# A two-layer graph network on one core: one group a step, PE's results read later, layer 1 summed in a PSUM bank

## The chip, the cores and the metric

The kernel runs on one core of a Trainium2 chip. The metric is device time in microseconds (us), the median of the runs. Engines are named as in the profile: PE (TensorE), PEld (its weight loads), DVE (VectorE), ACT (ScalarE), POOL (GpSimd), SP (SyncE, which here only issues DMAs).

## The reference

A graph has 12,500 nodes with 48 features and 200,000 edges sorted by destination. All numbers are float32.

```python
# layer 0
x_i, x_j = x[dst], x[src]
h = relu(concatenate([x_i, x_j, edge_attr_32], axis=1) @ W1 + b1)   # 128 hidden
msg = h @ W2 + b2                                                    # 48
x = layernorm(x + segment_sum(msg, dst))
# layer 1
m = relu(x[src] + edge_attr_48)
x = layernorm(x + (1 + eps) * x + segment_sum(m, dst))
```

## The kernel before, in words

The edges are cut into 391 groups of 512 (128 partitions x 4 tiles), and two groups make a pair; there are 196 pairs. A group's destinations lie close together, since the edges are sorted: a window of 48 nodes, with a start that is worked out on the chip, holds them all (should one fall outside, `check_windows` raises a flag and a general path runs; it doesn't here). The nodes are cut into 14 segments of 896.

In both layers POOL fetches the rows `x[src]` with indirect DMAs, one for each tile of 128 edges: `gather`, L187, 1564 times a layer.

Layer 0, for a pair `p`:
- `fetch0`: 8 gathers into `cat`, which has per edge 48 columns for a one-hot row, 48 for `x[src]`, 32 for the edge's features.
- `fill0`: ACT copies the edge features into `cat` (L391), DVE writes the one-hot rows (L276: which of the window's 48 nodes is this edge's destination), SP loads for each group the 48 rows of `x @ W1[0:48]` of its window (computed by `project`) into `wcat` (L394). So one matmul gives all three parts of the first linear layer.
- `turn0`: PE transposes the tiles of `cat` into PSUM tile `pt` (L402), DVE copies it to `cat_t` (L404).
- `hidden0`: PE multiplies `cat_t` by `wcat` into `ph` (L412), ACT adds the bias and applies relu (L416).
- `message0`: PE multiplies by W2 into `pm` (L423), DVE adds the bias and writes `msg` (L425).
- `sum0`: PE multiplies `msg` with the one-hot rows into `pa` (L309, 4 tiles added up for each group); `add0`: DVE adds `pa` into the segment's sums `agg` at a column read from a register (L302).

Layer 1, for a pair: `fetch1` gathers from the table of layer 0's results into `xs`; `fill1` writes the one-hot `hot` (L276) and loads edge features; `message1` adds on DVE (`m`, L491) and applies relu on ACT (L493); `sum1` and `add1` as in layer 0.

When a segment's last group has been added, `finish0` or `finish1` adds the overlaps of neighbouring segments, transposes the sums on PE (`px`, L325), and computes the layer norm on DVE and ACT; SP stores the result. Layer 1's gathers wait for all of layer 0's stores.

The order of the work is written out by hand. `run` (L438) goes through steps `k`; in each step it calls the listed stages, a stage with number `d` for pair `k - d`. Every engine executes its instructions in this order. Layer 0's list (L471) holds, with their numbers, fetch (-3), fill (-1), `message0` (1), `turn0` (0), `sum0` (1), `add0` (1), `hidden0` (0). So within one step DVE reads `pm` and `pt`, ACT reads `ph` and DVE reads `pa`, each as soon as PE has written it. In layer 1 (L508) `message1`, `sum1` and `add1` all have number 0. PSUM tiles are single (`bufs=1`); `cat` and `xs` have six buffers of a pair each, `hot` and the messages two, `wcat` four. A gather into a buffer waits until the buffer's last reader is done: `sum0` (PE) in layer 0, `m` (DVE) in layer 1.

```python
    run(
        [(fetch1, -AHEAD), (fill1, -1), (message1, 0), (sum1, 0), (add1, 0)],
        add1, finish1, lead1,
    )
```

Of the kernel before, what the change touches and what calls it, by code (L numbers as in the profile page):

```python
# [51 lines left out]
PAIRS = -(-NCHUNK // 2)  # L53
AHEAD = 3
NW = 4
EC = 6
# [3 lines left out]


def groups(p):
    return range(2 * p, min(2 * p + 2, NCHUNK))
# [27 lines left out]
def gnn_kernel(  # L91
# [18 lines left out]
    with ExitStack() as fast:  # L110
# [4 lines left out]
        min_val=0, max_val=2 * P,  # L115
# [5 lines left out]
def windowed(ctx, tc, dram, flag, x, src, dst, e32, e48, w1, b1, w2, b2, eps, out):  # L121
    nc = tc.nc
    const = ctx.enter_context(tc.tile_pool(name="const", bufs=1))
    cats = ctx.enter_context(tc.tile_pool(name="cats", bufs=AHEAD + 3))
    echunk = ctx.enter_context(tc.tile_pool(name="echunk", bufs=3))
    work = ctx.enter_context(tc.tile_pool(name="work", bufs=2))
    aggs = ctx.enter_context(tc.tile_pool(name="aggs", bufs=3))
    node = ctx.enter_context(tc.tile_pool(name="node", bufs=2))
    seg = ctx.enter_context(tc.tile_pool(name="seg", bufs=3))
    psum = ctx.enter_context(tc.tile_pool(name="psum", bufs=1, space=bass.MemoryType.PSUM))  # L130
# [52 lines left out]

    a_dram = [dram.tile([SROWS, HID], F32, name=f"a{s}", tag=f"a{s}") for s in range(NSEG)]
# [31 lines left out]

    begin.close()

    def check_windows():
        flat = rel.rearrange("p g t -> p (g t)")  # L220
        most = node.tile([P, 1], F32, name="most")
        nc.vector.tensor_reduce(most, flat, AX.X, ALU.max)
        least = node.tile([P, 1], F32, name="least")
        nc.vector.tensor_reduce(least, flat, AX.X, ALU.min)
        over = node.tile([P, 1], F32, name="over")
        nc.vector.tensor_scalar(over, most, float(W), None, op0=ALU.is_ge)
        bad = node.tile([P, 1], F32, name="bad")
        nc.vector.scalar_tensor_tensor(bad, least, 0.0, over, op0=ALU.is_lt, op1=ALU.add)
        pf = psum.tile([1, 1], F32, name="px")
        nc.tensor.matmul(pf, bad, ones[:P, 0:1], start=True, stop=True)  # L230
        nc.vector.tensor_copy(flag, pf)
# [27 lines left out]
    def load_edges(name, table, width, p):  # L259

        c, g = divmod(2 * p, EC)
        if g == 0:
            n = min(EC, NCHUNK - c * EC)
            chunk[name] = echunk.tile([P, EC * TPC, width], F32, name=name)
            nc.sync.dma_start(
                chunk[name].rearrange("p (c t) d -> p c (t d)", t=TPC)[:, :n, :],
                table[c * CHUNK * EC : (c * EC + n) * CHUNK, :].rearrange(
                    "(c p t) d -> p c (t d)", p=P, t=TPC
                ),
            )  # L270
        return chunk[name][:, g * TPC : (g + len(groups(p))) * TPC, :]

    def one_hot(o, p):
        n = len(groups(p)) * TPC
        r = rel.rearrange("p g t -> p (g t)")[:, 2 * p * TPC : 2 * p * TPC + n]
        nc.vector.tensor_tensor(  # L276
            o, iota_w[:, None, :].to_broadcast([P, n, W]),
            r[:, :, None].to_broadcast([P, n, W]), op=ALU.is_equal,
        )
# [4 lines left out]
    def start_of(engine, layer, g):  # L284
        if (engine, layer, g // 4) not in starts_of:
            kind = {nc.sync: mybir.EngineType.SP, nc.vector: mybir.EngineType.DVE}[engine]
            _, starts_of[engine, layer, g // 4] = nc.values_load_multi_w_load_instructions(
# [4 lines left out]
        return starts_of[engine, layer, g // 4][g % 4]  # L292
# [3 lines left out]
    def add_window(layer, g, pa):  # L296
        s = seg_of(g)
        if (layer, s) not in agg:
            agg[layer, s] = aggs.tile([D, SROWS], F32, name="agg")
            nc.vector.memset(agg[layer, s], 0.0)  # L300
        cols = agg[layer, s][:, bass.ds(start_of(nc.vector, layer, g), W)]
        nc.vector.tensor_tensor(cols, cols, pa, op=ALU.add)  # L302

    def reduce_tiles(p, hot, msg):
        pa = psum.tile([D, 2, W], F32, name="pa")
        for i, g in enumerate(groups(p)):
            for j in range(TPC):
# [414 lines left out]
```

## Time and profile before

| | |
|---|---|
| runs | 4828.99, 4833.04 (median), 4858.2 us |
| the profiled execution's own time | 4849.45 us |
| its span | 4847.7 us |
| busy, of the span | PE 41%, PEld 31%, DVE 19%, ACT 9%, POOL 63% |
| first gather of layer 0, of layer 1, end of the last gather | 7.57, 2556.8, 4832.6 us |
| granted TensorE clock, 80 to 2600 us and 2600 us to the end | 0.69, 0.50 of full speed |

The page of the profile gives for each group of instructions: line, engine, operation, output and inputs by the program's names, shapes and count; then busy time and mean duration in ns; then the engine's idle time just before these instructions and what ended most of it ("issue": nothing that the profile shows; "remote": a semaphore whose writer the profile could not tell). In the timeline a row has start, duration, engine, line and operation, and in brackets the idle time before it. Busy time of PE is modelled. A row of windows has the stretch, its length, the busy time with the count, the granted clock, the DMA engines' share and GB/s. A row of waits has the engine and line that waited, whom for, the total in us, the number of times and the longest.

### The profile page before, as it was taken

The numbers are of one execution on the slowest core, as the hardware profiler recorded it, in microseconds if no ns is written. First come the engines' busy times: TensorE is split into PE (matmuls) and PEld (weight loads), VectorE is DVE, ScalarE is ACT, GpSimd is POOL, SyncE is SP. The second block draws the span as 40 slices with busy tenths as digits, with TensorE's granted clock in tenths as the row PEclk, the third lists the DMA queues.
The fourth block names the chain that finished last, engine by engine and source line by source line (L and its number), as shares of the span: only waits on it lengthen the run. The fifth ranks groups of instructions, "written<-read, shape, count | busy, mean of one in ns | idle before, by whom it ended". The sixth has DMA issues, their size and how long they took to land.

```text
span 4847.7 us, 37626 instructions
## 1 busy us (share of the span) xinstructions
PE 2000.8 (41%) x12224; PEld 1503.6 (31%) x12224; DVE 925.0 (19%) x2082; ACT 434.8 (9%) x702; POOL 3073.4 (63%) x3136
## 2 busy tenths in 40 slices
PE   4666666666667667666660111011111110111011
PEld 2454555444445445454540111011011110111011
DVE  1222222222222222222220111112111111121112
ACT  1111111111111111111110000000000000000000
POOL 6556665656655666655646766667666766676666
PEclk7767676766766666767675555555555555555555
DMA  2111111111111111111111121112111211221121
GB/s 50 34 37 36 30 40 37 30 36 37 30 37 37 33 37 37 30 37 36 30 27 37 30 44 38 33 28 45 40 31 30 46 39 19 43 44 39 18 44 35
DMA packets 296027, 172.52 MB, mean 36 GB/s; under 512 B 111040, under 2 KB 295568, under 8 KB 295824
## 3 DMA queue, kind: packets, MB, share of 16 engines
q0 software_dynamic: 100096, 77.07, 10.7%
q1 hardware_dynamic: 178832, 84.31, 6.4%
q10 hardware_dynamic: 16896, 8.69, 0.6%
q8 instruction: 97, 1.59, 0.1%
q14 instruction: 106, 0.87, 0.1%
HBM read 157.20 MB, written 12.62 MB: 35 GB/s over the span
## 4 chain that ended last, share of the span: by engine, by line
another core or an unknown queue 43%; PE 28%; issue 13%; DVE 5%; POOL 5%; ACT 3%; DMA 1%; DVEq 1%; ACTq 0%; SPq 0%; POOLq 0%
PE ph L412 9%; PE pm L423 7%; PE pa L309 6%; POOL xs L187 4%; PE pt L402 4%; ACT h L416 2%; DVE cat_t L404 1%; DVE m L491 1%; DVE agg L302 1%; PE px L243 1%; DVE msg L425 1%; PE px L325 1%; DVE cat L276 1%; ACT msg L493 0%
## 5 line engine op out<-in xcount | busy, mean ns | idle before, releaser
L187 POOL DMA_INDIRECT cat<-in_x_dram,src_i x1564 | 1521.5, 973 | 985.2 <-issue 973.9
L187 POOL DMA_INDIRECT xs<-x_dram,src_i x1564 | 1550.2, 991 | 773.4 <-issue 445.2
L309 PE MATMUL pa<-hot,msg 128*48 128x48 f32 x3128 | 296.3, 282 | 1821.0 <-issue 1116.1
L309 PEld LDWEIGHTS pa<-hot,msg 128*48 128x48 f32 x3128 | 264.8, 192 | 1852.5 <-issue 1134.7
L423 PE MATMUL pm<-w_sb,h 128*128 128x48 f32 x3128 | 530.8, 338 | 372.4 <-ACT h L416 233.6
L423 PEld LDWEIGHTS pm<-w_sb,h 128*128 128x128 f32 x3128 | 502.1, 252 | 576.9 <-ACT h L416 355.9
L412 PE MATMUL ph<-cat_t,wcat 128*128 128x512 f32 x782 | 546.6, 836 | 115.6 <-issue 66.1
L302 DVE TENSOR_TENSOR agg<-agg,pa 48x48 f32 x782 | 153.6, 196 | 2118.2 <-remote 1621.7
L416 ACT ACTIVATE h<-ph,b_sb 128x1024 f32<-128x1024 f32 x196 | 217.9, 1112 | 1939.6 <-PE ph L412 1400.6
L309 PE MATMUL pa<-cat,msg 128*48 128x48 f32 x3128 | 265.6, 263 | 270.1 <-DVE msg L425 207.7
L425 DVE TENSOR_TENSOR msg<-pm,b_sb 128x384 f32<-128x384 f32 x196 | 109.1, 556 | 1391.6 <-remote 543.4
L309 PEld LDWEIGHTS pa<-cat,msg 128*48 128x48 f32 x3128 | 236.8, 175 | 331.7 <-DVE msg L425 226.2
L402 PE MATMUL pt<-ident,cat 128*128 128x128 f32 x1564 | 328.8, 381 | 2.0 <-ACT cat L391 2.0
L402 PEld LDWEIGHTS pt<-ident,cat 128*128 128x128 f32 x1564 | 290.6, 214 | 2.3 <-ACT cat L391 2.3
L404 DVE COPY cat_t<-pt 128x1024 f32<-128x1024 f32 x196 | 239.0, 1220 | 232.5 <-PE pt L402 117.5
L493 ACT ACTIVATE msg<-m 128x384 f32<-128x384 f32 x196 | 102.2, 521 | 1916.3 <-DVE m L491 1475.8
L412 PEld LDWEIGHTS ph<-cat_t,wcat 128*128 128x128 f32 x782 | 183.1, 260 | 286.0 <-issue 221.3
L276 DVE TENSOR_TENSOR cat<-iota_w,rel 128x384 f32<-128x384 f32 x196 | 109.2, 557 | 36.7 <-issue 36.1
L491 DVE TENSOR_TENSOR m<-xs,e48c 128x384 f32<-128x384 f32 x196 | 106.6, 544 | 39.7 <-issue 19.2
L276 DVE TENSOR_TENSOR hot<-iota_w,rel 128x384 f32<-128x384 f32 x196 | 106.3, 543 | 0.3
L325 PE MATMUL px<-ident,agg 48*128 48x48 f32 x196 | 25.6, 291 | 188.4 <-DVE agg L319 93.1
L391 ACT ACTIVATE cat<-e32c 128x256 f32<-128x256 f32 x196 | 79.6, 406 | 42.6 <-DMA cat<-in_x_dram,src_i 14.7
(53 smaller groups left out, 325.5 us busy)
## 6 DMA issues: line engine op xcount, KB each, us to landing
e48c<-in_e_dram SPq DMA_DIRECT2D x65, 576.0 KB
cat<-in_x_dram,src_i POOLq DMA_INDIRECT x1564
xs<-x_dram,src_i POOLq DMA_INDIRECT x1564
e32c<-in_e_dram SPq DMA_DIRECT2D x65, 384.0 KB
wcat<-a SPq DMA_DIRECT2D x391, 24.0 KB
a<-a ACTq DMA_DIRECT2D x14, 256.0 KB
a<-a ACTq DMA_DIRECT2D x14, 192.0 KB
x_seg<-in_x_dram SPq DMA_DIRECT2D x14, 168.0 KB
```

The source lines that it names most:

```text
L187: nc.gpsimd.indirect_dma_start(out=t, out_offset=None, in_=table, in_offset=bass.IndirectOffsetOnAxis(ap=src_i[:, g * TPC + j : g * TPC + ...
L276: nc.vector.tensor_tensor(o, iota_w[:, None, :].to_broadcast([P, n, W]), r[:, :, None].to_broadcast([P, n, W]), op=ALU.is_equal,)
L302: nc.vector.tensor_tensor(cols, cols, pa, op=ALU.add)
L309: nc.tensor.matmul(pa[:, i, :], msg[:, k, :], hot[:, k, :], start=j == 0, stop=j == TPC - 1)
L402: nc.tensor.transpose(pt[:, k, :], cat[p][:, k, :], ident[:P, :P])
L404: nc.vector.tensor_copy(cat_t[:, :n, :], pt[:, :n, :])
L412: nc.tensor.matmul(ph[:, part_of, :], wcats[g % NW], h[p][:, part_of, :], start=True, stop=True)
L416: nc.scalar.activation(t[:, :n, :], ph[:, :n, :], AF.Relu, bias=b1_sb)
L423: nc.tensor.matmul(pm[:, k, :], h[p][:, k, :], w2_sb, start=True, stop=True)
L425: nc.vector.tensor_tensor(msg[:, :n, :], pm[:, :n, :], b2_sb[:, None, :].to_broadcast([P, n, D]), op=ALU.add)
L491: nc.vector.tensor_tensor(m[:, :n, :], xs[:, :n, :], h[p], op=ALU.add)
L493: nc.scalar.activation(msg[:, :n, :], m[:, :n, :], AF.Relu)
```

## The change

A step now handles one group, not a pair. In layer 0 the stages are split where PE's result is read, and the reader stands one step after PE: `turned0` (DVE copies `pt`), `relu0` (ACT reads `ph`), `bias0` (DVE reads `pm`), `add0` (DVE reads `pa`). `pt`, `ph` and `pm` have two PSUM tiles. `cat` has 14 buffers of one group, `xs` 10, `wcat` 8; the gathers stay six groups ahead in the order, and an edge chunk is five groups instead of six.

In layer 1 the window of a group no longer comes from a register: group `g` gets 128 fixed destinations from `32 g - 48` on (`rel1`), so that neighbouring groups' windows overlap by a known amount. PE adds 12 groups into one PSUM bank of 480 columns: a matmul with zeros opens it, each group's four tiles are added at column `32 i`, a matmul with zeros closes it. `drain1` stands nine steps after the group in the order (eight after its sum): DVE adds the bank's first 96 columns to the ring `table`, ACT copies the other 384. A segment is finished once its columns are complete. `hot` and `msg1` come from a pool of ten buffers. `check_windows` checks both kinds of window.

```diff
-AHEAD = 3
-NW = 4
-EC = 6
+AHEAD = 6
+NW = 8
+EC = 5
+R1 = 48
+GB = 12
...
+W1 = STEP + 2 * R1
+SB = GB * STEP
+BANK = SB + 2 * R1
+RING = 5 * SB
...
-    cats = ctx.enter_context(tc.tile_pool(name="cats", bufs=AHEAD + 3))
+    cats = ctx.enter_context(tc.tile_pool(name="cats", bufs=AHEAD + 8))
     echunk = ctx.enter_context(tc.tile_pool(name="echunk", bufs=3))
-    work = ctx.enter_context(tc.tile_pool(name="work", bufs=2))
+    xs_pool = ctx.enter_context(tc.tile_pool(name="xs_pool", bufs=AHEAD + 4))
+    late = ctx.enter_context(tc.tile_pool(name="late", bufs=10))
+    work = ctx.enter_context(tc.tile_pool(name="work", bufs=3))
...
+    rel1 = const.tile([P, NCHUNK, TPC], F32, name="rel1")
+    nc.vector.tensor_tensor(
+        rel1, dst_g, fixed[:, :, None].to_broadcast([P, NCHUNK, TPC]), op=ALU.subtract
+    )
...
+    def turn0(g):
+        pt[g] = psum.tile([Q, TPC, P], F32, name="pt", bufs=2)
+        for j in range(TPC):
+            nc.tensor.transpose(pt[g][:, j, :], cat[g][:, j, :], ident[:P, :P])
+
+    def turned0(g):
+        h[g] = work.tile([Q, TPC, P], F32, name="cat_t")
+        nc.vector.tensor_copy(h[g], pt.pop(g))
+
+    def hidden0(g):
+        ph[g] = psum.tile([HID, TPC, P], F32, name="ph", bufs=2)
+        nc.tensor.matmul(ph[g], wcats[g % NW], h[g], start=True, stop=True)
+
+    def relu0(g):
+        h[g] = work.tile([HID, TPC, P], F32, name="h")
+        nc.scalar.activation(h[g], ph.pop(g), AF.Relu, bias=b1_sb)
...
     run(
-        [(lambda p: p >= AHEAD and fetch0(p), -AHEAD), (fill0, -1), (message0, 1), (turn0, 0),
-         (sum0, 1), (add0, 1), (hidden0, 0)],
+        [(lambda g: g >= AHEAD and fetch0(g), -AHEAD), (fill0, -2), (add0, 7), (sum0, 6),
+         (bias0, 5), (message0, 4), (relu0, 3), (hidden0, 2), (turned0, 1), (turn0, 0)],
         add0, finish0, lead0,
     )
...
+    def fill1(g):
+        o = late.tile([P, TPC, W1], F32, name="hot")
+        nc.vector.tensor_tensor(
+            o, iota_1[:, None, :].to_broadcast([P, TPC, W1]),
+            rel1[:, g, :, None].to_broadcast([P, TPC, W1]), op=ALU.is_equal,
+        )
+        hot[g] = o
+        h[g] = load_edges("e48c", e48, D, g)
+
+    def message1(g):
+        m = work.tile([P, TPC, D], F32, name="m")
+        nc.vector.tensor_tensor(m, cat.pop(g), h[g], op=ALU.add)
+        msg = late.tile([P, TPC, D], F32, name="msg1")
+        nc.scalar.activation(msg, m, AF.Relu)
+        h[g] = msg
...
+    def sum1(g):
+        k, i = divmod(g, GB)
+        last = i == GB - 1 or g == NCHUNK - 1
+        if i == 0:
+            bank[k] = psum.tile([D, BANK], F32, name="pt", bufs=2)
+            nc.tensor.matmul(bank[k], zeros[:, :D], zeros[:, :BANK], start=True, stop=False)
+        o, msg = hot.pop(g), h.pop(g)
+        for j in range(TPC):
+            nc.tensor.matmul(
+                bank[k][:, i * STEP : i * STEP + W1], msg[:, j, :], o[:, j, :],
+                start=False, stop=False, skip_group_check=True,
+            )
+        if last:
+            nc.tensor.matmul(
+                bank[k], zeros[:, :D], zeros[:, :BANK], start=False, stop=True
+            )
+
+    def drain1(g):
+
+        k, i = divmod(g, GB)
+        if i < GB - 1 and g < NCHUNK - 1:
+            return
+        for first, end in (0, R1), (R1, 2 * R1):
+            at = (k * SB - R1 + first) % RING
+            if k * SB - R1 + first >= 0:
+                both = table[:, at : at + R1]
+                nc.vector.tensor_tensor(both, both, bank[k][:, first:end], op=ALU.add)
...
     run(
-        [(fetch1, -AHEAD), (fill1, -1), (message1, 0), (sum1, 0), (add1, 0)],
-        add1, finish1, lead1,
+        [(fetch1, -AHEAD), (fill1, -2), (sum1, 1), (drain1, 9), (message1, 0)],
+        None, None, lead1,
     )
```

## The prediction

> **What bounds the kernel now.** I read the page's fifth part first, then cut the span at the first and last gather of each layer, then read the waits of layer 1 and the timeline. The costliest rows are the gathers of L187, on POOL:
>
> ```profile
> L187 POOL DMA_INDIRECT cat<-in_x_dram,src_i x1564 | 1521.5, 973 | 985.2 <-issue 973.9
> L187 POOL DMA_INDIRECT xs<-x_dram,src_i x1564 | 1550.2, 991 | 773.4 <-issue 445.2
> ```
>
> The windows of L187 alone (length, busy time and count):
>
> ```profile
> 7.50:2509.10 2501.60, 1521.51 (x1564) 0.70 0.18 35
> 2509.10:2556.80 47.70, 0.00 (x0) 0.83 0.07 15
> 2556.80:4832.60 2275.80, 1550.15 (x1564) 0.50 0.18 36
> 4832.60:4847.70 15.10, 0.00 (x0) 0.50 0.08 16
> ```
>
> So the span is 7.5 + 2501.6 + 47.7 + 2275.8 + 15.1. In the timeline an undisturbed gather takes 0.94 to 0.95 us with 0.30 to the next: 1.25 us each, a floor of 1564 x 1.25 = 1955 us a layer. Layer 0 is 547 above it: 1521.5 - 1564 x 0.945 = 44 are stretched gathers, 2501.6 - 1521.5 - 1564 x 0.305 = 503 are pauses. Layer 1 by the same sums: 72 stretched, 249 paused.
>
> What makes POOL pause? The waits of layer 1:
>
> ```profile
> DVE agg L302 <- remote: 1521.6, 103, 41.6
> ...
> POOL xs L187 <- DVE m L491: 251.7, 38, 17.4
> ```
>
> POOL waits for a free `xs`, which `m` frees; `m` stands behind the window adds (L302) on DVE, and those sit idle up to 41.6 us. "Remote" hides what they wait for: their one wait on another engine is for `pa` from PE. The timeline near the start shows the effect bare:
>
> ```profile
> 50.62 3.65 PE L423 MATMUL pm<-w_sb,h 128*128 128x48 f32 x16 [7.70 <-ACT h L416]
> ...
> 54.06 1.93 PE L402 MATMUL pt<-ident,cat 128*128 128x128 f32 x8
> ...
> 67.29 0.94 POOL L187 DMA_INDIRECT cat<-in_x_dram,src_i  x1 [0.30 <-issue]
> 75.38 0.56 DVE L425 TENSOR_TENSOR msg<-pm,b_sb 128x384 f32<-128x384 f32 x1 [35.44 <-remote]
> 75.85 1.22 DVE L404 COPY cat_t<-pt 128x1024 f32<-128x1024 f32 x1
> ```
>
> `pm` ended at 54.27, its reader starts at 75.38, 7 us after POOL stopped: while gathers stream, PE's completion can reach other engines very late, and a whole burst then arrives at once. Pairing rows of the trace, 101 of 196 pairs in layer 1 have over 2 us between `pa` and its add; in layer 0 `msg` starts 1.7 us after `pm` on average. So: POOL is the floor, late PE results make it pause.
>
> **What the Trainium skill says.** "SBUF — State Buffer", section "SBUF: two separate sides": a DVE operation with two SBUF inputs holds the port pair shared with GpSimd, and a GpSimd operation that reads SBUF is shut out until it ends. The trace agrees:
>
> ```profile
> 3338.41 0.54 DVE L276 TENSOR_TENSOR hot<-iota_w,rel 128x384 f32<-128x384 f32 x1
> 3338.60 1.64 POOL L187 DMA_INDIRECT xs<-x_dram,src_i  x1 [0.30 <-issue]
> 3338.88 0.54 DVE L491 TENSOR_TENSOR m<-xs,e48c 128x384 f32<-128x384 f32 x1
> ```
>
> The gather that starts inside `hot` lasts 1.64, 0.69 more: until `m` ends (3339.42) less 0.12 after its own start. So a gather needs the port 0.12 us after its start, and two DVE operations back to back don't let it in between. "DMA: Bandwidth & Descriptors", section "SWDGE vs HWDGE vs iDMA": GpSimd writes the descriptors of indirect DMAs; no other engine can take this floor away (1.25 us here). "Perfetto Trace Analysis", section "Per-instruction lifecycle": a matmul's shown end is estimated and the semaphore's way isn't shown; 54.27 against 75.38 agrees, though the page says nothing of 20 us. "PSUM — Partial Sum Buffer", section "The four PSUM rules": a matmul that starts a group clears the bank's written marks, later ones add. That is what the zero matmul opens the 480-column bank for; no run shows it yet.
>
> **The change part by part.** *One group a step, layer 0.* The gathers stay 1564. DVE's four operations at half size stand in the groups with shapes kept apart (the odd last pair): one-hot 0.36, `msg` 0.36, `cat_t` 0.69, add 0.20 = 1.61 a group against 2.73 a pair now, 0.24 more a group, 96 us in all; ACT 0.69 + 0.30 against 1.52 a pair, 88 in all. Both lie under POOL (DVE busy 587 and ACT 317 of 2520 us) and cost nothing; without that cover they would cost those sums. PE does the same matmuls: (329 + 547 + 531 + 266)/391 = 4.3 us a group, under 5.0. SP loads the same 391 `wcat`, two steps ahead with eight buffers, and 79 edge chunks in place of 66; nothing waits for SP longer than for POOL. The added constants and the doubled window check (about 2 + 4 us of DVE) lie under the first gathers.
>
> *Results read a step later, two PSUM tiles each.* Step k's PE work needs only step k-1 of DVE and ACT, and these need only step k-1 of PE. The loop is two steps long: step >= (PE 4.3 + DVE 1.6 + hops 0.3 + lateness)/2, so lateness up to 3.8 us costs nothing against 5.0. Where PE is late by more, DVE stalls, but POOL has about six groups (30 us) of `cat` ahead (14 buffers, one freed at step g+6). What is late next: `project` and `finish0`, where PE and ACT or DVE still wait for each other in the same step, some 27 places. I take 60 us of pauses in place of 503; bounds 0 and 310 (5.8 us a group).
>
> *Collisions, layer 0.* One-hot still waits for the fourth gather of its group. Landings come about 2.2 us after a gather's start, the DVE waits add 0.13: it runs from 2.33 to 2.69 while the port is wanted at 2.50 + 0.12. That is 0.07 x 391 = 27, and 15 for the layer norms. Layer 0: 1955 + 27 + 15 + 60 = 2057.
>
> *Between the layers.* 47.7 now. The last group has nine steps to pass instead of two pairs, without POOL beside it: 50.
>
> *Layer 1.* Gone are 782 window adds with their 98 register loads, and every wait for PE in the step. `hot` grows to 512 elements: from 384 at 0.544 and 192 at 0.343, 0.68 us; `m` is 0.36. DVE 1.07 with the drain, against 0.74; hidden as such. PE moves 128 columns where it moved 48, at most 8 x 0.24 = 1.9 us (the slow `pt` rate), and 66 zero matmuls of 1.7 (L211's two rows, nearest in shape); hidden under 5.0. The drain stands eight steps (40 us) behind the last sum. A new wait: `hot` waits for the slot that the sums of seven steps ago read, with `m` behind it on DVE and POOL behind `m`; but 35 us of lateness and then nine `xs` slots lie in between. So I take no pause, bounds 0 and 249.
>
> The price is the port. `m` waits for the fourth gather's landing, `hot` follows at once: from 2.33, `m` takes 0.27 to the next start, `hot` 0.69, end at 3.29. The gather due at 2.50 wants the port at 2.62 and gets it at 3.29: 0.67 a group, locked in phase, 391 x 0.67 = 262. Bounds: 0, if `m` starts only after 2.62, and 0.96 x 391 = 375. Plus 15 for layer norms. Layer 1: 1955 + 262 + 15 = 2232, hardly below its 2276: the pause comes back as collisions.
>
> *Tail.* 15.1 now; now nine steps without work, closing matmul, drain, last segment: 22.
>
> Sum: 7.5 + 2057 + 50 + 2232 + 22 = 4369 of span against 4847.7, -9.9%. The profiled execution's own time is 4849.45, the median of the runs 4833.04, 0.34% lower: 4355.
>
> **Rivals.** *No collisions in layer 1*: landing and waits together last past 2.62, as in one pair of the trace (`m` at 2.76, after four waits in a row; here there are two). 4355 - 262 = 4093, say 4095. Against it: landings of 2.08 to 2.44 in most of the rows I looked at.
> *Late results still stop POOL*: layer 0 at 5.8 us a group (+208), or layer 1 keeps its 249. About 4570. For it: at the start, with POOL streaming without pause, results were 10, 6.5 and 21 us late; against it: with PE at work every 3.6 to 5.8 us (the burst from 3338 on) at most 2.3 us, and PE is busier now.
> *Slower*: the same lateness as a lasting state in layer 0. From (6.2 + lateness)/2, the kernel is slower than now once layer 0 exceeds 4848 - 7.5 - 50 - 2232 - 22 = 2537, or 6.5 us a group: mean lateness 6.8. At 9 us, 7.6 a group, 2972, and about 5270. Against it: then POOL pauses a third of the time, and pauses let results through.
>
> **How the numbers follow.** Forecast 0.60 (own range 4230 to 4480), no collisions 0.15, POOL still stopped 0.17, slower 0.08. The range must take in most of the second and third: 4070 to 4620. About 1% is what a measurement can tell from no change; of the third case 0.02 falls within it: faster 0.90, same 0.02, slower 0.08.
>
> **What would show it.** Windows of the gather line: layer 0 near 2060, layer 1 near 2230. Gathers of layer 0 with under 100 us of pauses; in layer 1 one of four gathers near 1.6 us, three at 0.94, busy time near 1740. DVE idle before `m` ended by gathers' landings, not by PE. Wrong, if POOL's pauses stay above 250 in a layer, if layer 1's gathers stay at 0.95 on average, or if PE's step exceeds 5 us.

## The result, and the profile after

| | before | after |
|---|---|---|
| median, lowest to highest of 17 runs each, us | 4837.81 (4818.58 to 4864.2) | 4818.23 (4791.39 to 4850.15) |
| the profiled execution's own time and span, us | 4849.45; 4847.7 | 4809.57; 4807.8 |

The ratio of after to before is 0.9952, with a 95% interval of 0.993 to 0.9974: half a per cent faster, where 10% was forecast. The same two rows of the page, now with the line number L205, and the groups that hold most of DVE's and ACT's waiting:

```profile
L205 POOL DMA_INDIRECT cat<-in_x_dram,src_i x1564 | 1485.9, 950 | 932.4 <-issue 725.4
L205 POOL DMA_INDIRECT xs<-x_dram,src_i x1564 | 1560.7, 998 | 799.1 <-issue 444.8
...
L489 DVE TENSOR_TENSOR hot<-iota,rel 128x512 f32<-128x512 f32 x391 | 267.7, 685 | 1067.6 <-remote 1034.9
...
L429 ACT ACTIVATE h<-ph,b_sb 128x512 f32<-128x512 f32 x391 | 268.0, 685 | 1849.1 <-remote 987.2
```

The windows of the gather line, cut at the first and last gather of each layer as before:

```profile
6.90:2421.30 2414.40, 1485.90 (x1564) 0.74 0.17 36
2421.30:2468.20 46.90, 0.02 (x1) 0.80 0.06 14
2468.20:4781.20 2313.00, 1560.73 (x1564) 0.56 0.16 35
4781.20:4807.80 26.60, 0.00 (x0) 0.63 0.05 10
```

By the sums of the prediction: layer 0 has 8 us of stretched gathers and 452 of pauses (44 and 503 before), layer 1 has 83 and 276 (72 and 249). Layer 0 gained 87 us, layer 1 lost 37, the tail lost 11. POOL still pauses for as long as before. The waits of layer 1 (3000 to 4700 us) show on what:

```profile
PEld pt L514 <- issue: 1174.8, 502, 28.6
PE pt L514 <- issue: 1045.1, 481, 28.4
DVE hot L489 <- remote: 737.0, 43, 32.6
...
POOL xs L205 <- DVE m L498: 208.5, 16, 24.1
```

`hot` waits for the slot that PE's sums hold, although that slot has seven steps to come free. And PE itself waits for nothing that the profile can name. In the timeline, its sums in the middle of the layer, with weight loads between them:

```profile
3286.55 0.37 PE L514 MATMUL pt<-hot,msg 128*48 128x128 f32 x1 [2.43 <-issue]
3289.36 0.37 PE L514 MATMUL pt<-hot,msg 128*48 128x128 f32 x1 [2.43 <-issue]
3292.16 0.37 PE L514 MATMUL pt<-hot,msg 128*48 128x128 f32 x1 [2.43 <-issue]
```

A group has 8 such matmuls (and 8 loads), all with their inputs ready; one starts every 2.8 us, so a group takes some 22 us where the gathers bring one in 5. I call a stretch slow in which six or more PE instructions follow one another at 0.6 to 4.4 us. There are 20 of them in layer 1, 1343 of its 2313 us, with 21 us a group on average, and nearly all distances in them are multiples of 0.70 us. The trace of before has none, though there too the adds stand up to 40.6 us behind PE's sums.

The trace also has the times at which PE's semaphore went up, which is what the readers wait for. In the rows of before that the prediction shows, nine increments (one for `pm`, eight for `pt`) are recorded from 75.36 us on, 0.034 us apart, though these matmuls end at 54.3 to 55.8 by the model. In a slow stretch of the changed kernel they are recorded 22.4 us apart (3136.66, 3159.09, 3181.52). So it is PE's own signal that is late, not the engine that reads it.

In layer 0 (500 to 2400 us):

```profile
ACT h L429 <- remote: 803.0, 119, 16.9
...
PE pa L327 <- DVE agg L322: 468.6, 99, 8.6
```

Pairing rows, each relu with the `ph` that it reads: 157 of 391 start over 2 us after PE's end and after ACT is free, 99 of them over 5 us; 111 bias additions over 2 us.

### The profile page after: what moved, and what is told of

The parts are those of the page before. It is cut to its first block, busy times and chain, and to the rows that moved or that the text cites. A ratio compares the mean times of both kernels' runs of the same rounds, so it can differ in the third digit from the quotient of the medians.

```text
span 4807.8 us, 39682 instructions
## 1 busy us (share of the span) xinstructions
PE 2397.4 (50%) x12358; PEld 1670.6 (35%) x12358; DVE 1039.8 (22%) x2698; ACT 553.4 (12%) x1326; POOL 3049.0 (63%) x3138
## 4 chain that ended last, share of the span: by engine, by line
issue 24%; POOL 24%; PE 22%; another core or an unknown queue 21%; DVE 2%; DMA 2%; ACT 2%; DVEq 0%; ACTq 0%; POOLq 0%; SPq 0%
POOL xs L205 23%; PE pm L434 7%; PE ph L425 6%; PE pa L327 3%; PE pt L417 3%; DMA xs<-x_dram,src_i 2%; PE pt L514 1%; PE px L266 1%; ACT cat L408 1%; POOL cat L205 1%; ACT h L429 1%; DVE msg L438 0%; PE px L335 0%; DVE agg L322 0%
## 5 line engine op out<-in xcount | busy, mean ns | idle before, releaser
L205 POOL DMA_INDIRECT cat<-in_x_dram,src_i x1564 | 1485.9, 950 | 932.4 <-issue 725.4
L205 POOL DMA_INDIRECT xs<-x_dram,src_i x1564 | 1560.7, 998 | 799.1 <-issue 444.8
L514 PE MATMUL pt<-hot,msg 128*48 128x128 f32 x3128 | 635.6, 341 | 1575.1 <-issue 1418.5
L514 PEld LDWEIGHTS pt<-hot,msg 128*48 128x48 f32 x3128 | 446.1, 153 | 1788.4 <-issue 1595.7
L489 DVE TENSOR_TENSOR hot<-iota,rel 128x512 f32<-128x512 f32 x391 | 267.7, 685 | 1067.6 <-remote 1034.9
L429 ACT ACTIVATE h<-ph,b_sb 128x512 f32<-128x512 f32 x391 | 268.0, 685 | 1849.1 <-remote 987.2
L421 DVE COPY cat_t<-pt 128x512 f32<-128x512 f32 x391 | 268.0, 686 | 617.1 <-PE pt L417 286.0
L500 ACT ACTIVATE msg<-m 128x192 f32<-128x192 f32 x391 | 141.5, 362 | 1570.5 <-DVE m L498 725.4
L438 DVE TENSOR_TENSOR msg<-pm,b_sb 128x192 f32<-128x192 f32 x391 | 138.0, 353 | 811.8 <-remote 353.5
L498 DVE TENSOR_TENSOR m<-xs,e48c 128x192 f32<-128x192 f32 x391 | 140.5, 360 | 564.9 <-DMA xs<-x_dram,src_i 522.2
L296 DVE TENSOR_TENSOR cat<-iota_w,rel 128x192 f32<-128x192 f32 x391 | 135.2, 346 | 0.1
L408 ACT ACTIVATE cat<-e32c 128x128 f32<-128x128 f32 x391 | 117.1, 300 | 49.2 <-DMA e32c<-in_e_dram 26.1
```

Source lines behind the costliest of these rows:

```text
L205: nc.gpsimd.indirect_dma_start(out=t, out_offset=None, in_=table, in_offset=bass.IndirectOffsetOnAxis(ap=src_i[:, g * TPC + j : g * TPC + ...
L408: nc.scalar.activation(cat[g][:, :, W + D :], e, AF.Copy)
L421: nc.vector.tensor_copy(h[g], pt.pop(g))
L429: nc.scalar.activation(h[g], ph.pop(g), AF.Relu, bias=b1_sb)
L489: nc.vector.tensor_tensor(o, iota_1[:, None, :].to_broadcast([P, TPC, W1]), rel1[:, g, :, None].to_broadcast([P, TPC, W1]), op=ALU.is_equal,)
L498: nc.vector.tensor_tensor(m, cat.pop(g), h[g], op=ALU.add)
```

## Experiments

The kernels ran on several chips, each beside the kernel before on the same chip. Which chip it was turned out to matter more than any edit that keeps the computation whole: on five of eight the kernel before takes 4807 to 4849 us, as in its first trace, on the other three 3983 to 3987. I call the first kind late, the second punctual. A time without an interval is that of one execution, the profiled one. Lengths of layers are from the first to the last gather; pauses are what lies between gathers beyond 0.305 us. The kernel before differs by up to 42 us among the late chips, so differences of that size between rows from different chips show nothing.

Of the runs, one has no result: deeper buffers all at once (e3: 22 for `cat`, 17 for `xs`, 18 for `hot` and `msg1`) don't fit into SBUF. What depth is worth was then asked in e10, e12 and e14.

| run | chip, before | time | layer 0, pauses | layer 1, pauses |
|---|---|---|---|---|
| before, first trace | late | 4849 | 2502, 504 | 2276, 249 |
| after, first trace | late | 4810 | 2414, 452 | 2313, 276 |
| e5 after again | punctual 3983 | 3973 | 1960, 0 | 1961, 0 |
| e6 before again | late 4849 | 4844 | 2506, 505 | 2260, 227 |
| e7 before + lag | late 4849 | 5485 | 3100, 1131 | 2269, 236 |
| e8 after + lag | late 4849 | 4966 | 2571, 609 | 2314, 269 |
| e13 readers in the same step | late 4807 | 5040 | 2595, 639 | 2327, 288 |
| e10 second pa; deeper layer 1 | late 4843 | 4775 | 2372, 411 | 2316, 272 |
| e12 deeper cat; two banks | late 4807 | 4804 | 2391, 434 | 2319, 304 |
| e14 second pa and deeper cat | late 4814 | 4769 | 2356, 399 | 2310, 274 |

**PE kept busy in layer 1 (e1), and the changed kernel itself (e5).**

```diff
+    def warm1(g):
+        pw = psum.tile([HID, TPC, P], F32, name="ph", bufs=2)
+        for _ in range(2):
+            nc.tensor.matmul(pw.rearrange("p a b -> p (a b)"), ident, spare, start=True, stop=True)
...
-        [(fetch1, -AHEAD), (fill1, -2), (sum1, 1), (drain1, 9), (message1, 0)],
+        [(fetch1, -AHEAD), (fill1, -2), (sum1, 1), (warm1, 1), (drain1, 9), (message1, 0)],
```

> The changed kernel with two more matmuls a group in layer 1 (a 128x128 identity by 512 columns of ones, into a PSUM tile that nobody reads), so that PE has no long idle stretches. In the trace of the changed kernel PE goes through layer 1 in stretches of 70 to 100 us in which one PE instruction (weight load or matmul) starts only every 0.70, 1.40 or 2.10 us although its inputs are there: 1343 of 2313 us, all at a granted clock of 0.5. Theory 1 (such stretches come when PE is idle between groups, at the low clock): they are gone or nearly so, POOL pauses below 80 us in layer 1 (276 now), layer 1 of 2050 to 2150 us in place of 2313. Rival (they come from the gathers or from this form of sum, whatever PE does besides): the stretches stay, the added matmuls are drawn out too, and layer 1 takes 2313 or more.

It took 3968.77 us, beside 3986.73 for the kernel before: a punctual chip, so the run says nothing on the theory. So the changed kernel was run unchanged:

> The changed kernel itself, once more. In the last call the kernel before took 3986.7 us, not 4833, and the kernels with extra matmuls and with gathers that nobody reads showed no late PE result at all. Theory 1 (late results are a property of the chip or of a state that it is in, not of a program): where the kernel before takes about 3987 us again, the changed one takes 3965 to 3975 us, POOL without a pause; where the kernel before takes about 4830, the changed one takes 4790 to 4850 with late results as in its first trace. Rival (the extra matmuls of layer 1 took the lateness away): beside a kernel before at 3987 the changed kernel still takes 4300 us or more, with slow stretches of PE in layer 1.

Another punctual chip: 3973.35 us beside 3983.24. The first theory held, the rival fell. The windows of the gathers (from 7.2 and from 1990 us on):

```profile
7.20:1967.00 1959.80, 1483.42 (x1564) 0.79 0.23 45
1967.00:1990.00 23.00, 0.48 (x1) 0.65 0.03 4
1990.00:3950.00 1960.00, 1482.08 (x1562) 0.51 0.21 42
```

1564 gathers in 1960 us, 1.25 each: the floor of 1955 to within 5 us, in both layers. No bias addition and no relu starts over 0.4 us late, and PE has no slow stretch, at a clock as low (0.51) as on the late chip (0.56). A low clock alone is not the cause. On such a chip the kernel before has little to lose either (3983), and the change is worth 10 us (one execution of each).

**Plain loads instead of gathers, and gathers that nobody reads (e2, e4; then e9 and e11 on late chips).**

```diff
-        for j in range(TPC):
-            gather(cat[g][:, j, W : W + D], x, g, j)
+        row = min(g * STEP, N - CHUNK)
+        nc.sync.dma_start(cat[g][:, :, W : W + D],
+            x[row : row + CHUNK, :].rearrange("(p t) d -> p t d", p=P))
```

> The changed kernel without gathers: each group's 512 rows come in one plain DMA from SP, from 512 rows that lie one behind the other (the look-up by source is left out). Theory 1 (PE's results are late because POOL streams gathers): none of the readers of PSUM starts over 2 us after PE's end except at segment ends, no slow stretches of PE in layer 1; layer 0 then goes at the pace of PE and its readers, 3.2 to 4.5 us a group, 1250 to 1760 us, and layer 1 at about 2 us a group, 800 us. Rival (PE's results are late in this kernel whatever POOL does): as now 157 of 391 relus and 111 of 391 bias additions start over 2 us late, layer 0 stays above 2000 us, and PE's slow stretches stay in layer 1.

> As the kernel with plain loads, but POOL issues all the gathers too, into ten buffers that nobody reads, so that nothing can make POOL pause (the sums use the plain rows; the look-up by source is left out). Theory 1 (gathers without pause hold PE's results back): POOL streams at 1.25 us a gather, 1955 us a layer, and PE's lateness has nothing that ends it: readers of PSUM wait 10 to 40 us again and again, layer 0 takes far longer than 1955 (over 3000 us), and layer 1's PE goes at 1.3 us an instruction, 21 us a group, while POOL streams. Rival (only bounded lateness): layer 0 and layer 1 end with POOL, at about 2000 us each, 4050 in all.

On the punctual chip (before: 3986.73) they took 1872.96 and 4085.92 us. So POOL can stream both layers without one pause, and PE's results still come on time there: that gathers stream is not enough for late results. Then, on late chips:

> The changed kernel with two edits, one a layer, since the layers are apart in the trace. Layer 0: plain DMAs of 512 rows in the order in which they lie, in place of the gathers (the look-up by source is left out). Layer 1: two more 512-column matmuls a group, into a PSUM tile that nobody reads. By the kernel before beside it one sees the chip: about 4840 us where PE's results come late, about 3985 where they don't. On a chip with late results, theory 1 (the lateness needs gathers): layer 0 takes about 1300 us, as on the chip without late results, with no relu or bias addition over 2 us late; rival (such a chip's PE is late whatever POOL does): over 1700 us. Layer 1, theory 2 (PE's slow stretches come from its idle time and low clock): no slow stretches, POOL's pauses under 80 us in place of 276; rival (the gathers or the form of the sum are enough): slow stretches over 1000 us as before, pauses 200 us or more. On a chip without late results: layer 0 1300 us, layer 1 1958 us.

> The kernel that took 4086 us on a chip without late results, once more, hoping for one with them: plain DMAs feed the work (the look-up by source is left out), and POOL issues all gathers into ten buffers that nobody reads, so nothing makes POOL pause within a layer. On a chip where the kernel before takes about 4840 us, theory 1 (a held result comes through when POOL stops; the pauses are how the kernel moves on): while POOL streams its 1955 us of layer 0, the chain of layer 0 gets far less than 391 groups done, at over 8 us a group, and goes at 3 to 4 us a group once POOL has run out of gathers; layer 1 the same way, so the whole takes over 5200 us. Rival (results are late by some us, with or without a stop of POOL): the chain goes at about 6.2 us a group all along, layer 0 of about 2420 us and layer 1 at most 2320, 4800 in all. On a chip without late results: 4086 us again.

e9 took 3900.18 us (before: 4842.64). In its layer 0, without gathers, no relu and no bias addition starts over 0.4 us late, and the last relu ends at 1322 us; in e2, on the punctual chip, it ends at 1324. No gathers, no late results. The Trainium skill ("DMA: Bandwidth & Descriptors", section "SWDGE vs HWDGE vs iDMA") says that GpSimd builds the descriptors of its own DMAs, while those issued from SP are made in hardware; that plain DMAs from SP delay no result agrees with this being the difference, but the run doesn't single it out, since the number and the kind of the loads changed as well; and nothing in the page speaks of late results. In layer 1 the added matmuls removed every slow stretch, but the pauses grew to 506 us. The waits of its layer 1:

```profile
DVE hot L494 <- remote: 1061.6, 67, 32.7
...
PE ph L511 <- remote: 865.6, 67, 28.6
```

The second row is PE waiting on the semaphore that its own earlier matmul raises (the unread tile's slot): PE's completion comes late even to PE. Pauses without slow stretches, here and in the kernel before (249 us in layer 1), say that the stretches are not what makes results late; that both have one cause is likely, but not shown. Of e9's theory 2 the first half held (no slow stretches), and the half that matters, fewer pauses, fell.

e11 took 5937.72 us (before: 4807.4), 1850 more than the same program on a punctual chip. The windows of the tile `ph`; the third pair of numbers, ACT's, counts relus of layer 0. In the first row POOL streams, in the second it has run out of gathers:

```profile
100.00:2177.00 2077.00, 63.28 (x62) 16.90 (x62) 21.28 (x31) 0.50 0.14 21
2177.00:3373.00 1196.00, 405.28 (x712) 112.47 (x712) 244.72 (x357) 0.93 0.29 65
```

31 groups in 2077 us, 67 us each, against 357 in 1196, 3.35 each. The same in layer 1 (windows of its relu): 139 groups in 2177 us, then 252 in 379.

```profile
3374.00:5551.00 2177.00, 50.36 (x139) 0.52 0.17 32
5551.00:5930.00 379.00, 91.14 (x252) 0.87 0.49 136
```

In e4, the same program on a punctual chip, 376 relus fall into the first of these windows. This is the mechanism as far as the runs show it: on a late chip PE's work hardly moves while POOL issues gathers at full pace. The pauses in the traces of before and after are not a loss that better buffering could hide: without them, as e11 shows, the work hardly moves.

**The kernel before again, and results made late on purpose (e6, e7, e8).** The lag, in both kernels at `pt`, `ph` and `pm`:

```diff
+    def lag(t, p):
+        one = tiny.tile([1, 1], F32, name="one")
+        nc.scalar.activation(one, p[0:1, TPC - 1, 0:1], AF.Copy)
+        nc.sync.dma_start(t[0:1, 0, 0:1], one)
```

> The kernel before itself, profiled in the state of the chip that this call gets. Theory 1 (its 752 us of POOL pauses come from late PE results alone, and these from the chip's state, not from the kernel's order): about 3985 us, POOL under 40 us of pauses in all, the readers of pm start within 0.2 us of PE's end or of their engine being free. Rival (part of the pauses belongs to the order of the kernel before, since PE's results are read in the same step): pauses of 100 us or more remain in one of the layers, and the fall against 4833 comes from elsewhere.

> The kernel before with every result of pt, ph and pm in layer 0 made late on purpose: ACT copies one element of it, SP writes it by DMA into the tile that the reader will overwrite, so the reader has to wait for that DMA, some 2.5 us after PE's end. Theory 1 (read in the same step, a late result stands in the loop: pm 2.0 to 3.6, lag 2.5, msg 0.56, cat_t 1.2, ph 2.2 to 3.8, lag 2.5, h 1.1, hops): 12.5 to 16 us a pair in place of 10, layer 0 of 2450 to 3150 us, POOL pauses of 500 us or more. Rival (the buffers ahead take it up): layer 0 stays under 2050 us.

> The changed kernel with the same lag of some 2.5 us at pt, ph and pm in layer 0. Theory 1 (the prediction's loop: a step takes at least (PE 4.3 + readers 1.6 + hops 0.3 + lag 2.5)/2 = 4.4 us, under the 5.0 of the gathers): nothing is lost, layer 0 of 1955 to 1990 us, no pauses of POOL beyond 30 us. Rival (reading a step later doesn't help against lateness, as the first result of the changed kernel seems to say): layer 0 of 2200 us or more.

All three fell on a late chip; e6 only repeats the first trace there. The lag costs layer 0 of the kernel before 594 us (3100 - 2506), that of the changed kernel 157 (2571 against 2414 in its first trace, on perhaps another chip). Each run by itself came out in the range expected for e7 and on the rival's side for e8, since the chip's own lateness was there as well. By the difference, reading a step later does give tolerance, as meant. It is not clean: the copy by which the lag is made stands on ACT in PE's own step, so that e8 reads PE's results there too (ACT stood 547 us before that copy between 500 and 2400 us, for a signal that the profile could not name), and a lag on a punctual chip was not measured.

**Readers back in the same step (e13).**

```diff
-        [..., (fill0, -2), (add0, 7), (sum0, 6),
-         (bias0, 5), (message0, 4), (relu0, 3), (hidden0, 2), (turned0, 1), (turn0, 0)],
+        [..., (fill0, -2), (message0, 1), (bias0, 1),
+         (turn0, 0), (turned0, 0), (sum0, 1), (add0, 1), (hidden0, 0), (relu0, 0)],
```

> The changed kernel with layer 0's readers back in the step of their PE work (the order of the kernel before, but with one group a step and the changed kernel's PSUM tiles and buffers); layer 1 is left as changed. Theory 1 (reading later is what gives tolerance; each result read at once puts its lateness into the loop two or three times a group instead of once or twice a pair): on a chip with late results layer 0 takes 2700 us or more, against 2414 changed and 2502 before; on one without, 3.6 to 5 us a group stand in the loop and it stays at 1960 to 2100. Rival (an equilibrium: POOL stops as long as it has to for results to come through, whatever the order): 2414 within 80 us.

Layer 0 took 2595 us, 181 over the changed kernel's first trace: between the two expectations. On the same chip e12, which has the changed order and deeper `cat` buffers, took 2391. So reading later is worth some 180 to 200 us at one group a step; but one group a step with readers in the same step is itself slower than pairs (2595 against 2502 to 2506, from other late chips). The net is the 87 of the result.

**Single pa, depth, two banks (e10, e12, e14).**

> The changed kernel with two edits, one a layer, and all of the computation. Layer 0: pa, the one PSUM tile left single, gets a second buffer (it lies behind pm in the same tile). Layer 1: xs 10 to 16 buffers, hot and msg1 10 to 14, so that 55 us of lateness are free in place of 35. On a chip with late results, theory 1 (the prediction overlooked that PE's sums, first in each step, wait for the add that must read the single pa of the step before: 480 us of PE's waits; so a pa that is 4 us late stops the loop): layer 0 falls from 2414 us by 100 to 300, to 2110 to 2310. Rival (lateness of ph and pt sets the pace too, and a pause lets results through, so POOL's pauses come back elsewhere): layer 0 within 60 us of 2414. Layer 1, theory 2 (in a slow stretch PE needs 21 us a group, four times the gathers' pace, so no finite depth helps): pauses 220 to 330 us as before. Rival (depth was too small by a little): below 150. On a chip without late results both layers stay at 1955 to 1965 us.

> The changed kernel with two edits, one a layer, and all of the computation. Layer 0: cat 14 to 20 buffers. Layer 1: the sums of the tiles go in turn to two PSUM banks (pt and ph), which the drain adds up, so that a matmul never adds onto what the one of the tile before has just written. On a chip with late results, layer 0, theory 1 (the chain of PE and its readers sets the pace, POOL is held to it): depth buys nothing, within 40 us of 2414; rival (bursts that more buffers would bridge): 100 us or more saved. Layer 1, theory 2 (in a slow stretch each matmul waits for the end of the write before it, and that end is reported late): no slow stretches, or under a third of the 1343 us; whether the pauses fall with them shows if they are the cause of the 276 us. Rival (slow stretches have nothing to do with the bank): over 1000 us of them again. On a chip without late results both layers 1955 to 1970 us.

> The changed kernel with a second buffer for pa (behind pm in the same PSUM tile) and cat of 20 buffers, no other edit; all of the computation. On a chip with late results the two edits gave 42 and 23 us of layer 0 each by itself. Theory 1 (pa is a loop of one step of its own, depth nearly nothing): layer 0 of 2340 to 2380 us, layer 1 unchanged near 2315, 4740 to 4790 in all, 1.0 to 1.8% under the kernel before. Rival (once pa is free, depth can be used): layer 0 under 2300, the total under 4720. On a chip without late results: 3965 to 3980, within 0.5% of the kernel before.

Against the changed kernel's first trace, layer 0 is 42 us shorter with a second `pa` (e10), under the 100 expected and within the rival's 60: PE's wait of 469 us for the single tile (above) had only been the nearest of several. With 20 `cat` buffers it is 23 shorter (e12), and deeper buffers in layer 1 changed nothing (272 against 276), as theory said; none of this is more than late chips differ by. With two banks the slow stretches stayed (1311 us): that they come from the sum of one tile following that of the tile before in one bank is refuted (the two passes of each tile still share a bank). e14, timed, is 0.9909 of the kernel before (0.9873 to 0.9945), 4768.86 against 4814.09; that interval overlaps the changed kernel's own, so what its two edits add isn't clear of noise.

**Rests of POOL (e15 to e19).** An iota on POOL into a tile that nobody reads, after each gather or after the four of a group:

```diff
+    def rest(n):
+        nc.gpsimd.iota(scratch[:, :n], pattern=[[1, n]], base=0, channel_multiplier=0,
+                       allow_small_or_imprecise_dtypes=True)
...
             gather(cat[g][:, j, W : W + D], x, g, j)
+            rest(256)
```

> The changed kernel with short rests of POOL: in layer 0 one iota of 256 columns after each gather (about 0.35 us and its issue, four times a group), in layer 1 two iotas of 512 columns after the four gathers of a group (about 1.3 us once a group). On a chip with late results, theory 1 (results are held as long as POOL issues gathers at its full pace, a little air lets them through): no reader over 5 us late, no slow stretches, and POOL's other pauses fall under 100 us a layer; each layer is then 1955 + 391 x 1.4, about 2500 us. Rival (only a stop that lasts past the last landing, some 3 us, lets results through): the rests are added to what is lost already, readers late by 5 to 9 us stay, pauses besides the rests stay above 250 us, and the layers take 2700 us or more. On a chip without late results: about 2500 us a layer.

On a late chip (before: 4814) it took 4790.67 us. In the timeline of layer 0 a gather now comes every 1.49 us:

```profile
1501.50 0.95 POOL L205 DMA_INDIRECT cat<-in_x_dram,src_i  x1 [0.16 <-issue]
1502.46 0.36 POOL L404 IOTA scratch<- 128x256 f32 x1
1502.98 0.96 POOL L205 DMA_INDIRECT cat<-in_x_dram,src_i  x1 [0.16 <-issue]
```

and keeps that pace: beyond it layer 0 has 8 us of pauses. No relu is over 3.1 us late (7 over 2), no slow stretch is left. In its layer 1 (2600 to 4700 us) nearly all of DVE's waiting is for landings; the longest wait that names PE is 2.6 us:

```profile
ACT msg L509 <- DVE m L507: 1852.7, 338, 7.9
DVE m L507 <- DMA xs<-x_dram,src_i: 1676.9, 330, 7.3
```

A rest of a third of a microsecond a gather, or of 1.2 a group, lets PE through; no long stop is needed. Layer 0 (2339 us) is even shorter than the changed kernel's 2414, but layer 1 is longer (2397 against 2313): there the rests cost more than the pauses had. How little is enough?

> The changed kernel with smaller rests of POOL: in layer 0 an iota of 128 columns (about 0.23 us) after each gather, in layer 1 one iota of 512 columns (0.6 us) after the four gathers of a group. With rests of 0.37 a gather and 1.2 a group no result was over 3.1 us late, on a chip where the kernel before takes 4814; a gather followed by an iota takes 0.96 + iota + 0.16 in place of 1.25. Theory 1 (any stretch in which POOL issues no gather lets held results through, the length matters little): no lateness, layer 0 of 1564 x 1.35 = 2111 us, layer 1 of 391 x 5.5 = 2140, about 4330 in all on a chip with late results. Rival (there is a pace beyond which results are held, between 1.25 and 1.49 us a gather on average): late results are back, 4500 us or more.

> The same with rests of another size: in layer 0 an iota of 16 columns after each gather (some 0.15 us, so that a gather comes every 1.27 us, hardly less often than without), in layer 1 one of 128 columns after each gather. Theory 1 (it is enough that POOL does something else between two gathers): layer 0 of 1990 to 2020 us without late results, layer 1 of about 2111, 4200 in all on a chip with late results. Rival (the pace counts): layer 0 stays at 2300 us or more, only layer 1 is free of late results.

> The kernel before with an iota of 128 columns after each gather in both layers, nothing else changed. Theory 1 (with rests the late results are gone, and then the order of the kernel doesn't matter, since everything hides under POOL): 2111 us a layer, about 4300 in all on a chip where it takes 4810 without rests, as near as the changed kernel with the same rests. Rival (the results stay late by 1 to 3 us, which the kernel before has in its loop and the changed one not): layer 0 of 2300 us or more.

| late chip, before 4831 | time | layer 0: rest, length, further pauses | layer 1: rest, length, further pauses |
|---|---|---|---|
| e16, after | 4719.06 | 128 columns a gather, 2381, 210 | 512 a group, 2273, none for PE |
| e17, after | 4778.35 | 16 a gather, 2425, 414 | 128 a gather, 2286, 107 |
| e18, before | 4789.91 | 128 a gather, 2441, 268 | 128 a gather, 2263, 90 |

Further pauses are what goes beyond the gathers' own median distance with the rest (1.38 us with 128 columns, 1.28 with 16), counted where a gather comes over 0.3 us late. In layer 0 the rivals held in all three runs. With 128 columns (e16) the further pauses are half of 452, but the lateness is not: 98 of 391 relus are over 5 us late, as many as without rests (99), against none with 256 columns (e15). In e16 the rests had mostly taken the place of pauses: what lies between gathers beyond 0.305 us, rests included, sums to 399 us there, 447 in e17 and 362 in e15, against 452. With the same rest on the same chip the changed order is still worth 60 us of layer 0 (e16 against e18).

One rest of 0.58 us a group does more in layer 1 than four of a quarter microsecond: e17 still has 389 us of slow stretches there and e16 none. In e16 `m` waits for landings alone, and what layer 1 has above 1.36 us a gather is one gather a group stretched by the DVE port (1624.6 us busy, 147 over 1564 x 0.945); whether that stretch is part of the help was not separated. e16 is the fastest version that was run on a late chip, 0.977 of the kernel before (one execution each). Last, a version put together from this:

> The changed kernel with a second buffer for pa (behind pm) and rests of POOL at the pace that the runs so far point to: in layer 0 an iota of 192 columns after each gather (about 1.44 us from gather to gather), in layer 1 one of 512 columns a group (1.40 on average). All of the computation. Theory 1 (on a chip with late results there is a pace, between 1.40 and 1.49 us a gather, up to which results come on time; what the kernel adds in pauses fills up to it): layer 0 of 2260 to 2330 us with under 60 us of pauses, layer 1 of 2265 to 2280, 4600 to 4680 in all, 3 to 5% under the kernel before and below each version so far. Rival (pauses and rests add up, whatever the pace): 4750 or more. On a chip without late results: about 4530 in all, 13% over the kernel before.

It fell on a punctual chip: 4576.38 us beside 3984.55, ratio 1.1485 (1.1466 to 1.1504). There the rests are pure loss. On a late chip this version was not run, nor one with a single rest a group in layer 0; whether either beats e16 there stays open.

## Why the prediction was wrong

**What bounds the kernel now.** Right in its parts, POOL as floor and late PE results as the cause of its pauses. What it did not ask is what ends a hold. It says "PE's completion can reach other engines very late", and takes this as a delay that a reader can be moved away from. e11 shows it is no delay of given length: with POOL at full pace a group takes 67 us, without gathers 3.35.

**The step that failed, layer 0: "so lateness up to 3.8 us costs nothing against 5.0 ... I take 60 us of pauses in place of 503".** The pauses were 452. The span came out 439 us over the sum of 4369: pauses +392 in layer 0 and +276 in layer 1, collisions and layer norms -34 and -194, the rest -1. The size of the lateness came from one burst in layer 1 ("at most 2.3 us"), where POOL had just stopped (3.09 us idle before 3336.11); in layer 0, 113 of 391 relus were over 3.8 us late and 99 over 5. "Step k's PE work needs only step k-1" also overlooked the single `pa`, for whose add PE waits in the same step; e10 puts that at some 42 us, no more than late chips differ by. That readers a step later tolerate more was right in kind (e7 and e8, with the reserve said there, and e13).

**The step that failed, layer 1: "35 us of lateness and then nine xs slots lie in between. So I take no pause".** 276 us. No step after PE waits for PE soon, but in the slow stretches PE itself needed some 21 us a group, so 35 us of slack are used up after a few groups, and 55 are too (e10). The second rival described both layers, but told them as either-or and had a chance of 0.17: with both, 4355 + 208 + 249 is 4812, near the 4818.23 measured, if partly by luck: those two pauses fell short by 184 and 27, and most of the collisions did not come, which made up for it.

**Collisions.** Layer 0: 42 forecast with layer norms, 8 measured. Layer 1: 277 forecast, 83 measured, and 7 in e5. Here too a step failed: "The gather due at 2.50 wants the port at 2.62 and gets it at 3.29". It assumes that `m` comes first, at 2.33. In e5 `m` starts 2.55 us after its fourth gather (the median), just after the next gather, and in 229 of 391 cases within 0.12 us of that gather's start. None of these 229 gathers is stretched:

```profile
3005.85 0.94 POOL L205 DMA_INDIRECT xs<-x_dram,src_i  x1 [0.30 <-issue]
3005.95 0.36 DVE L498 TENSOR_TENSOR m<-xs,e48c 128x192 f32<-128x192 f32 x1 [3.94 <-DMA xs<-x_dram,src_i]
```

So a gather that has started before `m` keeps the port: `m` doesn't get in during the 0.12 us that the prediction left it, and the 262 us of the sum mostly fell away. The Trainium skill ("SBUF — State Buffer", section "SBUF: two separate sides") says that whichever starts first has the port for its whole instruction, and this agrees. "Two DVE operations back to back don't let it in between" is wrong as a rule as well. In the changed kernel's own trace:

```profile
3220.31 0.36 DVE L498 TENSOR_TENSOR m<-xs,e48c 128x192 f32<-128x192 f32 x1 [6.05 <-DMA xs<-x_dram,src_i]
3220.39 1.10 POOL L205 DMA_INDIRECT xs<-x_dram,src_i  x1 [0.30 <-issue]
3220.59 0.69 DVE L489 TENSOR_TENSOR hot<-iota,rel 128x512 f32<-128x512 f32 x1
```

The gather is 0.16 us longer than usual: it waits for the end of `m` (3220.67, less the 0.12), not for that of `hot` (3221.28). But in the trace of before, where `m` follows `hot`, a gather that starts inside `hot` does wait for the end of `m`, 74 times of 77; and in the changed kernel one that started at 3206.09 lasted 8.99 us, beside nine `m` and as many `hot` without a gap on DVE. What decides at such a border, neither the page nor a run says. In e16, where the rest shifts the phase so that the gather starts inside `hot`, the locked collision did come, 0.37 us a group.

**Tail and crossing.** 26.6 and 46.9, for 22 and 50. The busy times of the half-size operations were right (`msg` 0.36, `cat_t` 0.69, `hot` 0.68, `m` 0.36), and a zero matmul took 0.72 us for each of its two passes.

What stays open: why five of the eight chips of the experiments have late results and three not, what the 0.70 us are, and why a rest between gathers lets PE through. Each chip has one set of runs only, so that it is the chip, and not a state that it was in, isn't shown. No run touches the cause inside the chip.

## What to carry to other kernels

Before moving readers away from a late result, ask what ends the lateness: here, on a late chip, it was the pauses of the engine that waits last, POOL, so every order of the work settled at 1.45 to 1.66 us a gather, and only air between the gathers (0.36 us each in layer 0, or 0.58 once a group in layer 1) made results come on time. That air costs about as much as the pauses did, and on a punctual chip it is a loss of 15%. A lateness read off one burst is not a bound; pair all rows. And run the kernel before on another chip before explaining a stall: some 850 us of 4840 went with the chip.

## What the runs showed of the hardware

Of the eight chips of the experiments, five give the kernel before 4807 to 4849 us and three 3983 to 3987. On the late ones PE's completions are held while POOL issues gathers 0.305 us apart, even from PE itself (866 us in e9), and then recorded in a burst (nine within 0.3 us at 75.36 in the trace of before); and PE can slow to one instruction each 0.70 to 2.8 us (1343 us in layer 1 of the changed kernel, 221 in layer 0 of e10). The hold is gone when the issue of gathers is broken by other POOL work of 0.36 us after each (layer 0 of e15) or of 0.58 after four (layer 1 of e16), but not by 0.26 after each (layer 0 of e16). On the punctual ones 1564 gathers without a pause delay no relu and no bias addition by more than 0.4 us (e4, e5).
